# Three bias additions of GpSimd per graph, each in four pieces of 128x256 instead of one of 128x1024

## The chip, the cores and the metric

The kernel runs on one core of a Trainium2 chip, as one launch. The metric is the device time of the launch in microseconds (us). Three timed runs of the kernel before gave 2971.67, 2972.38 and 2974.36 us; the median is 2972.38 us. The profile that is read below is of one further execution.

## The reference

For each of 32 graphs there are node features `x` (512 nodes x 256, f32), an adjacency matrix `adj` (512x512, f32) and a node mask. Four graph layers follow each other, each with a residual and a layer norm:

```python
x = _layernorm(x + gin(x, adj))        # h = (1+eps)*x + adj@x; relu(h@W1 + b1)@W2 + b2
x = _layernorm(x + gat(x, adj))        # 4 heads, masked by adj > 0.5, softmax, ... + bias
x = _layernorm(x + attention(x, adj))  # 8 heads, scores + log(adj + 1e-6), softmax, (...)@Wo.T + bo
x = _layernorm(x + gnn3(x, mask, adj)) # (x@W)@x.T * adj, masked softmax, @x
```

The first three layers end in the addition of a row of 256 values: `b2`, `bias` and `bo`. These rows are the bias additions meant here. They are added to `x` itself, ahead of the layer's own result.

## The kernel before

**Tiling.** A graph's `x` is a tile of 128 partitions x 4 blocks x 256 columns, so node number c*128+p lies in block c of partition p. All of `x` is 128x1024 elements. The layers' matrices are held in transposed form where a matrix product needs them so. TensorE does all products and transposes, ScalarE (ACT in the profile) the exponentials and most copies out of PSUM, VectorE (DVE) the masking, statistics and residuals, GpSimd (POOL) the bias additions, the reciprocal square root of the norms, and the issue of accumulating DMAs between SBUF tiles. SyncE (SP) issues the loads and stores.

**Order.** Each graph is a list of named steps with an engine, an assumed duration, the steps that it comes after, and the buffers it takes. A planner (`Plan.order`) goes through the steps of all 32 graphs, up to six of them open at a time, and puts them into one order per engine by due times with hand-set shifts. The steps are then written out in that order, so every engine runs its own queue in order, and waits on semaphores of the others. Several graphs at different layers are in work at the same time: what stands next to each other on an engine is mostly of different graphs. The planner's assumed duration of a bias step is 2.5 us and is no part of the change.

**Names and lines used below.**
- L584, step `xb1`, `xb2`, `xb3` (one each per graph, `bias_steps(k, after)`): GpSimd adds row k-1 of `bias_bc` to all of `x`. `xb1` comes after the products that read `x` in layer 0 (L715, `hT_ps`), `xb2` after the transposes of `x` for layer 1 (L785, `xT_t`), `xb3` after those for layer 2 (L1057). The bias is added once nothing of the layer reads the plain `x` any more.
- L587 and L588: statistics of the norm, on VectorE. L604: `ve`, the variance plus epsilon, a 128x4 tensor-scalar operation on VectorE. L610: `rstd`, the power of -0.5 of it on GpSimd, 128x4. L618: `shift`, a 128x4 scalar-tensor-tensor operation on VectorE which needs `rstd`. L628: the normalization of `x` on ScalarE, which needs `shift`.
- L897: `edge`, the comparison of the transposed adjacency with 0.5, 128x512 f32 to uint8, on VectorE.
- L920: the combination of the layer-1 weights `z` with `T` and `edge`, 128x512, on VectorE. L943: the products that use `z` of layer 1 (`o_ps`).
- L1126: exponentials of layer 2 on ScalarE. L1135: their multiplication by the adjacency, 128x1024, on VectorE. L1171: the products that use them (`o_ps` of layer 2). L1113: the layer-2 scores.
- L971 and L1146: the accumulating DMAs that GpSimd issues.

Of the kernel before, what the change touches and what calls it, by code (L numbers as in the profile page):

```python
# [14 lines left out]
ALU = mybir.AluOpType  # L15
AX = mybir.AxisListType

P = 128
# [28 lines left out]
class Plan:  # L47
# [31 lines left out]
    def step(self, name, eng, us, after=(), take=(), free=(), mode=""):  # L79


        def add(emit):
            steps = self.steps[-1]
            known = {**steps, **{f"^{n}": s for n, s in self.steps[0].items()}}
            assert name not in steps and all(a in known for a in after), (name, after)
            takes = []
            for b in take:
                kind, _, key = b.partition("=")
                key, _, rest = key.partition("/")
                takes.append((kind, key or kind, int(rest or 0)))  # L90
            steps[name] = Step(eng, us, dict.fromkeys(after), takes, mode, emit)
            for b in free:
                self.free(b, (name,))
            return emit

        return add
# [131 lines left out]
def fast_path(  # L228
# [23 lines left out]
    nc = tc.nc  # L252
    B, N, D = x.shape
    NC = N // P
# [42 lines left out]
    bias_bc = const.tile([P, 3, D], F32, name="bias_bc")  # L297
# [259 lines left out]
    def graph(g):  # L557
# [3 lines left out]
        t = {"g": g}  # L561
# [16 lines left out]
        def bias_steps(k, after):  # L578


            @step(f"xb{k}", "pool", 2.5, after + ("^bias",))
            def _():
                b = bias_bc[:, k - 1, None, :].to_broadcast([P, NC, D])
                nc.gpsimd.tensor_tensor(t["x"], t["x"], b, ALU.add)  # L584

        def norm_stats(n, c):
            nc.vector.bn_stats(t[f"st{n}"][:, c, :], t["xo" if n == 4 else "x"][:, c, :])  # L587
# [1302 lines left out]
```

## Time and profile before

| what | value |
|---|---|
| median of the timed runs | 2972.38 us |
| the profiled execution, its own time | 2971.27 us |
| its span, first to last instruction | 2969.4 us |
| TensorE busy | 2943.3 us, 99% of the span |
| VectorE busy | 2150.4 us, 72% |
| ScalarE busy | 1927.3 us, 65% |
| GpSimd busy | 801.4 us, 27% |
| granted TensorE clock | 0.997 |
| bias additions | 96, shortest 2342 ns, median 2556 ns, longest 3246 ns |

The time of the execution is 1.9 us longer than its span. The span has a filling part at its start, when fewer graphs are open, a long middle part in which the same pattern of 91.3 us comes back for every graph, and a draining part. Profile lines have the start in us from the span's start, the duration in us, the engine, the line, the operation, the tiles (written <- read), their shapes, and, in brackets, the time that the engine sat idle before it and what ended the wait. A line with x2 or more merges instructions that follow each other.

### The profile page before, as it was taken

The numbers are of one execution on the slowest core, as the hardware profiler recorded it, in microseconds if no ns is written. First come the engines' busy times: TensorE is split into PE (matmuls) and PEld (weight loads), VectorE is DVE, ScalarE is ACT, GpSimd is POOL, SyncE is SP. The second block draws the span as 40 slices with busy tenths as digits, with TensorE's granted clock in tenths as the row PEclk, the third lists the DMA queues.
The fourth block names the chain that finished last, engine by engine and source line by source line (L and its number), as shares of the span: only waits on it lengthen the run. The fifth ranks groups of instructions, "written<-read, shape, count | busy, mean of one in ns | idle before, by whom it ended". The sixth has DMA issues, their size and how long they took to land.

```text
span 2969.4 us, 42791 instructions
## 1 busy us (share of the span) xinstructions
PE 2943.3 (99%) x15521; PEld 1668.0 (56%) x15521; DVE 2150.4 (72%) x4133; ACT 1927.3 (65%) x3818; POOL 801.4 (27%) x688
## 2 busy tenths in 40 slices
PE   8999999999999999999999999999999999999998
PEld 6545555555556555555555555555655555554545
DVE  3677777777777777677676777777777767767777
ACT  4666665667666676666676666766667666667664
POOL 1323222223232322222222222323232222223220
PEclk9999999999999999999999999999999999999999
DMA  4677766677766686666776666776668666677680
GB/s 146 137 156 174 165 153 140 145 158 169 166 146 140 140 183 162 154 134 143 176 165 155 137 148 156 170 166 146 139 140 185 159 156 133 142 176 157 138 178 16
DMA packets 153368, 448.93 MB, mean 151 GB/s; under 512 B 15232, under 2 KB 55360, under 8 KB 125248
## 3 DMA queue, kind: packets, MB, share of 16 engines
q0 software_dynamic: 63648, 295.73, 51.4%
q1 hardware_dynamic: 88112, 149.75, 15.4%
q8 instruction: 125, 2.05, 0.3%
q10 hardware_dynamic: 1392, 0.66, 0.1%
q14 instruction: 91, 0.75, 0.1%
HBM read 133.30 MB, written 17.07 MB: 51 GB/s over the span
## 4 chain that ended last, share of the span: by engine, by line
PE 85%; DVE 13%; DMA 1%; ACT 0%; issue 0%; POOL 0%; POOLq 0%; SPq 0%; ACTq 0%
PE h1T_ps L738 8%; PE s L1314 8%; PE hT_ps L715 8%; PE o_ps L1368 7%; PE y_ps L757 7%; PE o_ps L1171 6%; PE s L1113 6%; PE o_ps L943 5%; DVE z L1135 4%; PE v_ps L806 4%; PE v_ps L1094 4%; PE iT_ps L1300 4%; PE kT_ps L1076 4%; PE qT_ps L1076 4%; DVE st L587 2%; PE d_ps L1201 2%
## 5 line engine op out<-in xcount | busy, mean ns | idle before, releaser
L1126 ACT ACTIVATE z<-s 128x512 f32<-128x512 f32 x1024 | 551.3, 605 | 250.2 <-PE s L1113 250.0
L1135 DVE SCALAR_TENSOR_TENSOR z<-AT,z 128x1024 f32<-128x1024 f32 x512 | 625.6, 1241 | 95.7 <-ACT z L1126 93.0
L920 DVE SCALAR_TENSOR_TENSOR z<-z,T,edge 128x512 f32<-128x512 f32 x512 | 416.8, 857 | 38.2 <-ACT z L909 38.1
L1146 POOL DMA_DIRECT2D z<-z x186 | 164.1, 884 | 1005.5 <-DMA z<-z 358.7
L909 ACT ACTIVATE z<-R_bc,nT,S 128x512 f32<-128x512 f32 x512 | 376.6, 807 | 31.6 <-PE y_ps L757 22.4
L1220 DVE RECIPROCAL rdT<-rdT 128x256 f32<-128x256 f32 x128 | 215.9, 1725 | 188.3 <-ACT rdT L1213 188.3
L584 POOL TENSOR_TENSOR x<-x,bias_bc 128x1024 f32<-128x1024 f32 x96 | 245.2, 2555 | 395.0 <-PE xT_t L785 247.3
L971 POOL DMA_DIRECT2D z<-z x256 | 224.4, 970 | 457.0 <-DMA z<-z 168.4
L628 ACT ACTIVATE x<-x,shift,rstd 128x256 f32<-128x256 f32 x508 | 296.9, 600 | 52.1 <-DVE shift L618 51.5
L1171 PE MATMUL o_ps<-z,v 128*32 128x512 f32 x2048 | 295.3, 603 | 3.6 <-DVE z L1135 0.6
L1113 PE MATMUL s<-qT,kT 32*128 32x512 f32 x2048 | 288.1, 634 | 2.9 <-ACT qT L1082 2.9
L943 PE MATMUL o_ps<-z,v 128*64 128x512 f32 x1024 | 250.0, 609 | 2.7 <-DVE z L920 2.4
L738 PE MATMUL h1T_ps<-hT,w_sb 128*128 128x512 f32 x512 | 248.5, 610 | 0.0
L610 POOL TENSOR_TENSOR rstd<-ve,nhalf 128x4 f32<-128x4 f32 (+1 forms) x131 | 169.7, 1298 | 289.5 <-DVE ve L604 286.9
L1314 PE MATMUL s<-xT,iT 128*128 128x512 f32 x512 | 237.8, 599 | 0.0
L1368 PE MATMUL o_ps<-x,eT 128*128 128x256 f32 x1024 | 237.0, 379 | 0.1
L757 PE MATMUL y_ps<-w_sb,h1T 128*128 128x256 f32 x1024 | 230.8, 379 | 0.0
L757 PEld LDWEIGHTS y_ps<-w_sb,h1T 128*128 128x128 f32 x1024 | 194.2, 190 | 49.7 <-issue 25.8
L1368 PEld LDWEIGHTS o_ps<-x,eT 128*128 128x128 f32 x1024 | 193.8, 190 | 40.0 <-issue 13.6
L587 DVE BATCH_NORM_STATS2 st<-x 128x6 f32<-128x256 f32 x508 | 209.3, 412 | 4.7
L715 PE MATMUL hT_ps<-AT,x 128*128 128x384 f32 (+2 forms) x768 | 209.8, 382 | 0.0
L1113 PEld LDWEIGHTS s<-qT,kT 32*128 32x128 f32 x2048 | 87.2, 183 | 170.3 <-ACT z L1126 74.9
(152 smaller groups left out, 4236.8 us busy)
## 6 DMA issues: line engine op xcount, KB each, us to landing
z<-z POOLq DMA_DIRECT2D x186, 1024.0 KB, 8.7
A<-in_adj_dram SPq DMA_DIRECT2D x256, 256.0 KB
z<-z POOLq DMA_DIRECT2D x128, 512.0 KB, 5.5
R_bc<-R_dram SPq DMA_DIRECT2D x32, 1024.0 KB
z<-z POOLq DMA_DIRECT2D x128, 256.0 KB, 3.8
x<-in_x_dram SPq DMA_DIRECT2D x32, 512.0 KB
out_dram<-x SPq DMA_DIRECT2D x31, 512.0 KB
nm<-in_nodemask_dram SPq DMA_DIRECT2D x32, 256.0 KB
```

The costliest lines, as they stand in the source:

```text
L715: nc.tensor.matmul(ph[:, cols], t["x"][:, m, blk(d)], moving, start=(k == 0), stop=(k == len(parts) - 1),)
L738: nc.tensor.matmul(ph, w1_sb[:, d, blk(f)], t["hT"][:, d, :], start=(d == 0), stop=(d == DC - 1))
L757: nc.tensor.matmul(py[:, j, :], t["h1T"][:, f, blk(2 * c2 + j)], w2_sb[:, f, :], start=(f == 0), stop=(f == HC - 1),)
L909: nc.scalar.activation(t[f"e{h}"][:, c, :], t["Rbc"][:, h, :], AF.Relu, bias=t["nT"][:, h, c : c + 1], scale=t["S"][:, h, c : c + 1],)
L920: nc.vector.scalar_tensor_tensor(z, z, t["T"][:, h, c : c + 1], t["edge"][:, c, :], op0=ALU.add, op1=ALU.mult)
L943: nc.tensor.matmul(po[j * F1 : (j + 1) * F1, :], t["v"][:, c, h * F1 : (h + 1) * F1], t[f"e{h}"][:, c, :], start=(c == 0), stop=(c == NC - 1),
L1113: nc.tensor.matmul(pk, t["k"][hs, o, blk(c)], t["q"][hs, o, :], start=True, stop=True)
L1126: nc.scalar.activation(t[f"E{k}"][:, j, :], t[f"ps{k}{j}"], AF.Exp, scale=QSCALE)
L1135: nc.vector.scalar_tensor_tensor(z, t["AT"][:, c, None, :].to_broadcast([P, 2, N]), ADJ_EPS, z, op0=ALU.add, op1=ALU.mult,)
L1171: nc.tensor.matmul(t[f"n{o}"][32 * j : 32 * j + 32, :], t["v2"][:, c, o * P + F2 * j : o * P + F2 * (j + 1)], t[f"E{k}"][:, j, :], start=( ...
L1314: nc.tensor.matmul(pt, t["iT"][:, d, blk(c)], t["xT3"][:, d, :], start=(d == 0), stop=(d == DC - 1),)
L1368: nc.tensor.matmul(py, t[f"eT{c}"][:, blk(m)], t["x"][:, m, :], start=(m == 0), stop=(m == NC - 1),)
```

## The change

The one instruction of a bias step becomes a loop over the four blocks of `x`. Each piece reads and writes one block of 256 columns and reads the 256 values of the row directly, with no broadcast over blocks. The step keeps its name, its place, its predecessors and its assumed duration, so the planner gives the same order. Other lines move down by 3.

```diff
             @step(f"xb{k}", "pool", 2.5, after + ("^bias",))
             def _():
-                b = bias_bc[:, k - 1, None, :].to_broadcast([P, NC, D])
-                nc.gpsimd.tensor_tensor(t["x"], t["x"], b, ALU.add)
+
+                for c in range(NC):
+                    nc.gpsimd.tensor_tensor(
+                        t["x"][:, c, :], t["x"][:, c, :], bias_bc[:, k - 1, :], ALU.add
+                    )
```

In the built programs of this part GpSimd has 96 x 3 = 288 more additions. The four pieces stand where the one stood, and the order of all other instructions on all engines is the same. A piece waits for the last readers of its own block alone: for `xb2` and `xb3`, piece c waits for the transpose of block c, where the one addition waited for the transposes of all blocks. An instruction with several semaphores to wait for has a separate wait instruction ahead of it on its queue, and GpSimd has 235 more of those.

## Prediction

> **What bounds the kernel now.** I read the page first: busy times, the chain that ended last, and the row of the changed instruction.
>
> ```profile
> PE 2943.3 (99%) x15521; PEld 1668.0 (56%) x15521; DVE 2150.4 (72%) x4133; ACT 1927.3 (65%) x3818; POOL 801.4 (27%) x688
> ...
> PE 85%; DVE 13%; DMA 1%; ACT 0%; issue 0%; POOL 0%; POOLq 0%; SPq 0%; ACTq 0%
> ...
> L584 POOL TENSOR_TENSOR x<-x,bias_bc 128x1024 f32<-128x1024 f32 x96 | 245.2, 2555 | 395.0 <-PE xT_t L785 247.3
> ```
>
> TensorE is full, and GpSimd, which does the additions, is 27% busy and absent from the chain. That alone would say "no effect". But the chain runs through VectorE for 13% of the span, so I went through TensorE's timeline for places where a matmul starts later than the one before lets it. From 230 to 2700 us there is one such place, in every 91.3 us period. I read it in the graph around 1124 us, first GpSimd, then VectorE, then TensorE, each from its timeline.
>
> ```profile
> 1124.42 2.35 POOL L584 TENSOR_TENSOR x<-x,bias_bc 128x1024 f32<-128x1024 f32 x1 [8.50 <-PE xT_t L785]
> 1128.08 2.25 POOL L610 TENSOR_TENSOR rstd<-ve,nhalf 128x4 f32<-128x4 f32 x2 [1.31 <-DVE ve L604]
> ...
> 1124.77 2.02 DVE L604 TENSOR_SCALAR ve<-mv 128x4 f32<-128x4 f32 x1
> 1126.71 1.21 DVE L1135 SCALAR_TENSOR_TENSOR z<-AT,z 128x1024 f32<-128x1024 f32 x1
> 1127.85 0.16 DVE L604 TENSOR_SCALAR ve<-mv 128x4 f32<-128x4 f32 x1
> 1127.92 0.41 DVE L897 TENSOR_SCALAR edge<-AT 128x512 uint8<-128x512 f32 x1
> 1128.25 1.21 DVE L1135 SCALAR_TENSOR_TENSOR z<-AT,z 128x1024 f32<-128x1024 f32 x1
> 1129.39 0.41 DVE L897 TENSOR_SCALAR edge<-AT 128x512 uint8<-128x512 f32 x1
> 1129.72 0.15 DVE L618 SCALAR_TENSOR_TENSOR shift<-mv,rstd 128x4 f32<-128x4 f32 x1
> ...
> 1131.34 0.41 DVE L897 TENSOR_SCALAR edge<-AT 128x512 uint8<-128x512 f32 x1
> 1131.67 2.52 DVE L1135 SCALAR_TENSOR_TENSOR z<-AT,z 128x1024 f32<-128x1024 f32 x2
> ...
> 1131.80 0.60 PE L1171 MATMUL o_ps<-z,v 128*32 128x512 f32 x2
> ...
> 1132.94 1.05 PE L1171 MATMUL o_ps<-z,v 128*32 128x512 f32 x4
> ```
>
> The reader is to see two things. The first L604 works on 128x4 elements and takes 2.02 us, where the second takes 0.16: it stands still until the bias addition, which began 0.35 us earlier, ends at 1126.77. And from there to 1132.89 VectorE runs without a gap (each start lies some 0.08 us ahead of the end before), so the lost 1.9 us arrive whole at the first of the two L1135 at 1131.67. It ends at 1132.89, and the products that need it start 0.05 us later. The pair of matmuls before them started at 1132.23, and pairs of this line elsewhere follow each other by 0.42 us: TensorE loses 0.28 us. This repeats in 27 graphs, 27 x 0.28 = 7.6 us. Other steady waits of TensorE on VectorE have 0.4 us to spare or more. The stalls of the filling part, which add up to some 15 us, wait for layer chains where few graphs are open; I leave them as they are.
>
> **What the Trainium skill says.** "SBUF — State Buffer", section "Who interferes with whom": VectorE and GpSimd share a read and a write port, held for a whole instruction; an operation with two SBUF inputs, or a tensor-scalar operation in a two-port mode, blocks against a GpSimd operation that reads SBUF, and the one that started first holds. The trace agrees: L604 above, and L920 (0.74 us alone) takes 2.77 us in each `xb3`. Statistics (L587), with one input, lose nothing beside a bias addition. It also shows the other direction: at 252.72 us an addition waits for L920 and takes 2.94 us. "GPSIMD Engine Reference", section 3.1, gives 4497 ns for such an addition of 2048 columns. "Perfetto Trace Analysis", section "GPSIMD Engine Instruction", calls GpSimd spans unreliable and prefers start-to-start times; here the two bias additions that follow at 44.43 us take 4.67 us together, twice 2.36 less 0.05, so spans serve.
>
> **The change, part by part.**
>
> *Removed:* 96 additions of 2.35 us when undisturbed. *Added:* 384 pieces. The trace has no piece. With a fixed part f, a piece is f + (2352 - f)/4 = 588 + 0.75f ns. f is not below 0: 588 ns. An estimate for the upper end from the skill's 4497 ns and the 2352 here: slope (4497-2352)/1024 = 2.095 ns, f = 207, a piece 743 ns. The smallest GpSimd operations in the trace, fills of one column, take 97 to 102 ns; f = 100 gives 663. I take 700, so four take 4 x 0.70 - 3 x 0.05 = 2.65 us alone, 0.3 more than before. GpSimd, idle for 73% of the span, has room for it. The 235 added wait instructions are 17 ns each when fulfilled, and run ahead on the queue while the piece before works: nothing.
>
> *Moved:* the first piece may start three transposes earlier, 3 x 0.109 = 0.33 us before the addition did.
>
> *What matters is who gets the ports between pieces.* From the trace: a waiting addition gets them 0.14 us before the VectorE operation's end (252.72: 0.59 us of waiting, L920 ends at 0.72), ahead of VectorE's next, which already stood in line. VectorE gets them about 0.13 us before an addition's end. So they take turns. I write the place above out by hand, in us from 1124.42, with 0.57 us of ports per piece:
> - piece 1 from -0.33, piece 2 from 0.32; L604 waits until 0.89, the first L1135 follows at 0.97
> - piece 3 asks at 0.97 too. If VectorE is first: L1135 to 2.18, piece 3 from 2.10 to 2.80
> - L604 at 2.67, then at 2.75 L897 and piece 4 ask at the same moment. If VectorE is first: L897 to 3.16, piece 4 to 3.78, second L1135 from 3.65 to 4.86
> - GpSimd's L610 is queued behind piece 4. It begins at 3.73 and needs the ports, which the second L1135 holds to 4.72; then 1.03 us, so `rstd` is there at 5.8
> - L618 follows at 5.85. Before, it started at 5.30 (1129.72)
>
> Behind L618 everything stands in VectorE's queue: L897, L1135, L618, L897, and the L1135 for which TensorE waits. ScalarE also waits for it, at L628. From there nothing of the bias is left, and the rest follows as before, 0.55 us later. TensorE has no slack there, so it loses 0.55 us more per graph: 27 x 0.55 = 14.9 us. The profiled execution would become 2971.27 + 14.9 = 2986.2; the median lies 1.1 us above that execution, so 2987.
>
> The two bounds of a piece give, with the same turns, 0.1 us (588 ns) and 0.65 us (743 ns): 3 and 18 us. Turns are what decides. Both are near ties: an addition starts 0.05 us before the end of the one ahead (44.43 us), and VectorE's next operation starts 0.06 us before the end of an addition that blocked a short one (L1135 at 1126.71 against 1126.77). VectorE is ahead by 10 ns. In the trace a VectorE operation that starts 17 ns ahead wins (an L920 beside the addition at 252.72), one that starts 66 ns behind loses (L604 at 1763.93). Hence I let it win.
>
> *The other two places.* `xb1` runs mostly while VectorE idles; its first L1135 waits 0.2 to 0.6 us today, and the next is bound by ScalarE. `xb3` at 1183.47 blocks L920 for 2.03 us; with turns, three L920 and L1336 share the same sum of waits, the bias ends some 1.2 us later, and the DMA issues behind it start 1.5 us after its end today because they wait for L920. The products that use these results have 2 us to spare. I cost both at nothing; without that cover a wait of 0.3 us would be 8 us.
>
> **The rivals.**
> 1. *GpSimd wins one of the two ties.* Then piece 4 is done at 3.4 and L610 starts ahead of the second L1135, or just waits for L897; `rstd` is there at 4.7, VectorE reaches L618 at about 5.15 and TensorE's wait shrinks by 0.15 to 0.28 us, 4 to 7.6 us in all: about 2966. For it: the ties are within 10 ns, and a start in the record need not be the moment of the request. The gain can't be larger, since that wait is all there is.
> 2. *Nothing.* Total port time is about the same, pieces are near 588 ns and L618 moves by less than 0.1 us: 2972 to 2975. For it: GpSimd has 0% of the chain. Against: L610 has no more than 0.5 us to spare behind the bias.
> 3. *Pieces that wait longer.* If L1135 also comes between pieces 1 and 2 or wait instructions open gaps of 0.1 us, `rstd` comes a whole L1135 later, 1.1 us: 27 x 1.1 = 30 us, 3002.
>
> That the change doesn't do what it says is excluded by the built program: 288 more additions, the same order.
>
> **How the numbers follow.** Forecast (VectorE wins both ties) 0.58, rival 1 0.25, rival 2 0.13, rival 3 0.04. The likeliest gives 2987; its own range is 2979 to 2992. The range reaches to rival 1 at the lower end, 2965, and to 2994 above. A difference under 0.2%, 6 us, can't be told from none. Rival 1 gives 4 to 7.6 us: 0.14 of its 0.25 is counted as faster, 0.11 as the same. The same: 0.11 + 0.13. Slower: 0.58 + 0.04.
>
> **What would show it.** In the changed profile: pieces of 0.65 to 0.75 us with L1135 between the second and third and L897 before the fourth; L604 at 0.6 us or less; L618 of the middle graphs 5.8 us after the place of the old start; the wait of TensorE at the second L1171 pair grown from 0.28 to 0.8 us; a period of 91.85 us. L618 earlier than 5.3 us, or a fourth piece directly behind the third, makes the forecast wrong. So does a new wait of TensorE near `xb1` or `xb3`.

## The result and the profile after

The changed kernel takes 2989.28 us (median of 4 runs, 2988.76 to 2990.03); the kernel before took 2972.03 us beside it (4 runs, 2970.98 to 2974.36). The ratio is 1.0057, 95% interval 1.004 to 1.0075: slower by 0.57%. The profiled execution's span went from 2969.4 to 2988.2 us, by 18.8 us.

The page of the changed kernel: busy times, the chain, and two groups. A group's numbers are busy us, mean ns of one, and the idle us of the engine ahead of it, with what ended most of it.

```profile
PE 2949.8 (99%) x15521; PEld 1668.9 (56%) x15521; DVE 2152.0 (72%) x4133; ACT 1927.9 (65%) x3818; POOL 929.2 (31%) x976
...
PE 89%; POOL 4%; DVE 4%; issue 1%; DMA 1%; ACT 0%; POOLq 0%; SPq 0%; ACTq 0%
...
L585 POOL TENSOR_TENSOR x<-x,bias_bc 128x256 f32<-128x256 f32 x384 | 360.9, 1034 | 360.2 <-PE xT_t L788 241.9
...
L1174 PE MATMUL o_ps<-z,v 128*32 128x512 f32 x2048 | 303.6, 603 | 13.9 <-DVE z L1138 13.9
```

GpSimd, with 0% of the chain before, now has 4%. Its busy time grew by 128 us, but that is no measure of the damage: the records include waits for the ports, and GpSimd still idles for 69% of the span. The products L1174 (L1171 before) idled 3.6 us in the old profile, 0.6 us of it for `z`, and now 13.9 us, all for `z`.

Both programs have the same 15521 matmuls in the same order. So I compared, one by one, the time from each matmul to the next, and summed the differences by their place in the period of 91.3 us, for the steady 27 graphs. Only two places lose: the products behind `xb2`, 10.7 us, and the products behind `xb1`, 8.4 us. The filling and the draining part gain 0.2 and 0.5 us.

**Behind `xb2`.** The timeline of the changed kernel in one graph, GpSimd, VectorE and TensorE together; L607 is L604 of before, L613 is L610, L621 is L618, L1138 is L1135, L900 is L897.

```profile
1222.15 4.09 POOL L585 TENSOR_TENSOR x<-x,bias_bc 128x256 f32<-128x256 f32 x4 [8.92 <-PE xT_t L788]
...
1222.93 0.67 DVE L607 TENSOR_SCALAR ve<-mv 128x4 f32<-128x4 f32 x1
...
1223.51 1.21 DVE L1138 SCALAR_TENSOR_TENSOR z<-AT,z 128x1024 f32<-128x1024 f32 x1
...
1224.65 0.69 DVE L607 TENSOR_SCALAR ve<-mv 128x4 f32<-128x4 f32 x1
...
1225.24 0.41 DVE L900 TENSOR_SCALAR edge<-AT 128x512 uint8<-128x512 f32 x1
...
1225.58 1.74 DVE L1138 SCALAR_TENSOR_TENSOR z<-AT,z 128x1024 f32<-128x1024 f32 x1
...
1226.20 3.00 POOL L613 TENSOR_TENSOR rstd<-ve,nhalf 128x4 f32<-128x4 f32 x2
...
1228.25 0.16 DVE L621 SCALAR_TENSOR_TENSOR shift<-mv,rstd 128x4 f32<-128x4 f32 x1 [0.59 <-POOL rstd L613]
...
1230.23 2.51 DVE L1138 SCALAR_TENSOR_TENSOR z<-AT,z 128x1024 f32<-128x1024 f32 x2
...
1231.49 1.05 PE L1174 MATMUL o_ps<-z,v 128*32 128x512 f32 x4 [0.50 <-DVE z L1138]
```

The reader is to see the turns. The four pieces start at 1222.15, 1222.85, 1223.53 and 1225.27; the third waits while L1138 has the ports, and the fourth while L900 has them. The first L613 starts only behind the fourth, meets the second L1138, and takes 2.01 us instead of 1.03. VectorE now has a gap of 0.59 us ahead of L621, where before it had none. What follows is as before, later, and the last products wait.

**Behind `xb1`.** The timeline of before, then of the changed kernel, for the same graph.

```profile
1239.47 0.86 POOL L1146 DMA_DIRECT2D z<-z  x1 [10.84 <-issue]
...
1240.03 2.68 POOL L584 TENSOR_TENSOR x<-x,bias_bc 128x1024 f32<-128x1024 f32 x1
...
1242.07 5.14 DVE L1135 SCALAR_TENSOR_TENSOR z<-AT,z 128x1024 f32<-128x1024 f32 x4 [1.89 <-ACT z L1126]
...
1246.64 1.92 PE L1171 MATMUL o_ps<-z,v 128*32 128x512 f32 x16
```

```profile
1246.95 0.86 POOL L1149 DMA_DIRECT2D z<-z  x1 [11.09 <-issue]
...
1247.51 3.09 POOL L585 TENSOR_TENSOR x<-x,bias_bc 128x256 f32<-128x256 f32 x4
...
1249.31 5.79 DVE L1138 SCALAR_TENSOR_TENSOR z<-AT,z 128x1024 f32<-128x1024 f32 x4 [1.89 <-ACT z L1129]
...
1253.89 2.32 PE L1174 MATMUL o_ps<-z,v 128*32 128x512 f32 x16
```

Here the bias addition starts 0.30 us before the DMA issue ahead of it ends. There are no turns at all: the four pieces are through in 3.09 us, at 1250.60, and the first L1138, which asked at 1249.31, takes 2.38 us and ends 1.09 us after them. The sixteen products stretch from 1.92 to 2.32 us.

### The profile page after: what moved, and what is told of

Same layout as the page of the kernel before. It is cut to its first block, busy times and chain, and to the rows that moved or that the text cites. A ratio compares the mean times of both kernels' runs of the same rounds, so it can differ in the third digit from the quotient of the medians.

```text
span 2988.2 us, 43288 instructions
## 1 busy us (share of the span) xinstructions
PE 2949.8 (99%) x15521; PEld 1668.9 (56%) x15521; DVE 2152.0 (72%) x4133; ACT 1927.9 (65%) x3818; POOL 929.2 (31%) x976
## 4 chain that ended last, share of the span: by engine, by line
PE 89%; POOL 4%; DVE 4%; issue 1%; DMA 1%; ACT 0%; POOLq 0%; SPq 0%; ACTq 0%
PE h1T_ps L741 8%; PE s L1317 8%; PE o_ps L1174 8%; PE hT_ps L718 8%; PE o_ps L1371 7%; PE y_ps L760 7%; PE s L1116 7%; PE o_ps L946 4%; PE v_ps L809 4%; PE v_ps L1097 4%; PE iT_ps L1303 4%; PE o2p_ps L1259 4%; PE kT_ps L1079 4%; PE qT_ps L1079 4%; DVE z L1138 2%; POOL x L585 2%
## 5 line engine op out<-in xcount | busy, mean ns | idle before, releaser
L1138 DVE SCALAR_TENSOR_TENSOR z<-AT,z 128x1024 f32<-128x1024 f32 x512 | 653.8, 1297 | 92.8 <-ACT z L1129 89.5
L585 POOL TENSOR_TENSOR x<-x,bias_bc 128x256 f32<-128x256 f32 x384 | 360.9, 1034 | 360.2 <-PE xT_t L788 241.9
L1149 POOL DMA_DIRECT2D z<-z x186 | 163.7, 882 | 972.3 <-DMA z<-z 363.7
L923 DVE SCALAR_TENSOR_TENSOR z<-z,T,edge 128x512 f32<-128x512 f32 x512 | 387.5, 800 | 35.8 <-ACT z L912 35.7
L1174 PE MATMUL o_ps<-z,v 128*32 128x512 f32 x2048 | 303.6, 603 | 13.9 <-DVE z L1138 13.9
L613 POOL TENSOR_TENSOR rstd<-ve,nhalf 128x4 f32<-128x4 f32 (+1 forms) x131 | 188.2, 1440 | 270.1 <-DVE ve L607 255.3
L1371 PEld LDWEIGHTS o_ps<-x,eT 128*128 128x128 f32 x1024 | 193.8, 190 | 39.7 <-issue 13.9
```

The lines of the kernel that those rows point to most:

```text
L585: nc.gpsimd.tensor_tensor(t["x"][:, c, :], t["x"][:, c, :], bias_bc[:, k - 1, :], ALU.add)
L923: nc.vector.scalar_tensor_tensor(z, z, t["T"][:, h, c : c + 1], t["edge"][:, c, :], op0=ALU.add, op1=ALU.mult)
L1138: nc.vector.scalar_tensor_tensor(z, t["AT"][:, c, None, :].to_broadcast([P, 2, N]), ADJ_EPS, z, op0=ALU.add, op1=ALU.mult,)
L1174: nc.tensor.matmul(t[f"n{o}"][32 * j : 32 * j + 32, :], t["v2"][:, c, o * P + F2 * j : o * P + F2 * (j + 1)], t[f"E{k}"][:, j, :], start=( ...
L1371: nc.tensor.matmul(py, t[f"eT{c}"][:, blk(m)], t["x"][:, m, :], start=(m == 0), stop=(m == NC - 1),)
```

## The experiments

All are made from the kernel before; "before" beside them had 2972.3 to 2972.6 us. In their profiles the lines are shifted; names in the text are those of before.

| kernel | us, median | ratio to before, 95% interval | TensorE behind `xb2` | behind `xb1` |
|---|---|---|---|---|
| changed kernel | 2989.28 | 1.0057 (1.0040 to 1.0075) | +10.7 us | +8.4 us |
| `xb2` alone in four pieces | 2983.59 | 1.0039 (1.0026 to 1.0053) | +10.8 | +2.1 |
| `xb1` alone in four pieces | 2975.68 | 1.0011 (1.0005 to 1.0018) | -0.3 | +3.6 |
| `xb3` alone in four pieces | 2971.71 | 0.9998 (0.9990 to 1.0006) | -0.3 | 0.0 |
| all three in halves | 2965.89 | 0.9980 (0.9972 to 0.9988) | -6.0 | +0.7 |
| `xb2` as 256 + 768 | 2963.59 | 0.9970 (0.9958 to 0.9982) | -7.5 | +0.3 |
| `xb2` in pieces behind `rstd` | 3003.02 | 1.0104 (1.0089 to 1.0120) | -20.2 | +43.3 |
| `xb2` in one piece, later | 2952.42 | 0.9933 (0.9920 to 0.9947) | -31.4 | +1.4 |
| `xb2` in four pieces, later | 2961.72 | 0.9960 (0.9947 to 0.9974) | -31.4 | -0.1 |
| `xb1` in pieces, its DMA issue behind it | 2970.72 | 0.9994 (0.9985 to 1.0002) | -0.2 | -0.1 |
| `xb1` in pieces, small addition ahead | 2975.82 | 1.0010 (1.0003 to 1.0016) | -0.3 | +6.6 |

The two right columns are the sums of TensorE's differences against the profile of before, made as above. They leave out the filling part, which varies by up to 2.4 us and is 4.1 to 5.9 us longer in the three kernels that move `xb2`, and the products L715, which lose 6.9 and 17.7 us in the two kernels with `xb2` later and nothing in the others.

**One place at a time.** Three kernels, each with this edit for one k (here `xb2`):

```diff
             def _():
+                if k == 2:
+                    for c in range(0, NC, 1):
+                        b = bias_bc[:, k - 1, None, :].to_broadcast([P, 1, D])
+                        part = t["x"][:, c : c + 1, :]
+                        nc.gpsimd.tensor_tensor(part, part, b, ALU.add)
+                    return
                 b = bias_bc[:, k - 1, None, :].to_broadcast([P, NC, D])
```

> Only the second bias addition of a graph (xb2) in four pieces. Theory (the rstd waits behind piece 4, and the second L1135 keeps the ports from it): the stall of TensorE behind z at the second L1171 goes from 0.28 to 0.67 us in each graph, as in the changed kernel, so about +10 us, 2982 to 2983. Rival (every piece costs GpSimd a fixed time, and each of the three additions bears a third of the loss): +5.8 us, 2978.

> Only the first bias addition (xb1) in four pieces. Theory (its pieces follow a DMA issue so closely that they overlap and don't give the ports back, and L1135 is kept out until all four have ended, 0.6 us later than before, with about 0.3 us to spare): +8 us, 2980, with new waits of 0.3 us behind z at L1171 in some 20 of 27 graphs, and the stall after xb2 still 0.28 us. My forecast's reckoning (2 us to spare): 0, 2972. Rival (a third each): +5.8 us.

> Only the third bias addition (xb3) in four pieces. Theory: its place has neither a product nor a rstd that is late, so 0 within 1.5 us. Rival (a third each): +5.8 us, 2978.

`xb2` alone costs 11.3 us and `xb3` nothing, as expected; the rival of a price per piece falls, since the same 96 added pieces cost 11.3 us, 3.4 us and nothing. `xb1` alone costs 3.4 us and not 8, with 14 losing graphs of the 21 compared below, not 20 of 27: the three sum up to 14.1 us, against 17 for the whole change. 2.7 us of the missing 3.2 are at the products behind `xb1`, where the two changes make each other's harm worse (8.4 us together, 2.1 and 3.6 alone). I took the 21 steady graphs in which `xb1` of before starts within the DMA issue ahead of it or right at its end (in the other six it starts 0.19 to 0.56 us later), and counted its start and end from one fixed matmul, 30 ahead of `xb1` in TensorE's order:

| kernel | start of `xb1`, median | duration | end | graphs in which TensorE loses over 0.05 us | sum of 21 |
|---|---|---|---|---|---|
| before | 4.92 us | 2.68 us | 7.60 us | - | - |
| `xb2` in pieces | 5.15 | 2.68 | 7.83 | 8 | 2.1 us |
| `xb1` in pieces | 4.94 | 3.08 | 8.02 | 14 | 3.6 us |
| changed kernel | 5.15 | 3.08 | 8.24 | 19 | 8.4 us |

Two shifts, 0.23 us (`xb1` starts later when `xb2` is in pieces; the DMA issue behind `xb2` and `rstd`, 0.24 us after the first L1171 products before, comes 0.98 us after them in the changed kernel) and 0.40 us (four pieces are longer than one). TensorE's loss is a plain difference: in 18 of the 19 losing graphs of the changed kernel it is the end of `xb1` less 7.85 us to within 0.04 us (in 17, to 0.005), for example 8.042: 0.191, 8.238: 0.392, 8.639: 0.794. Before, the median end was 7.60. So the products there had 0.25 us to spare; either shift alone stays mostly inside it, and both together do not.

**Halves.** The same edit for all k, in steps of two blocks:

```diff
+                if True:
+                    for c in range(0, NC, 2):
+                        b = bias_bc[:, k - 1, None, :].to_broadcast([P, 2, D])
+                        part = t["x"][:, c : c + 2, :]
+                        nc.gpsimd.tensor_tensor(part, part, b, ALU.add)
+                    return
```

> All three additions in two pieces of 128x512. Theory: a half takes about 1.27 us (estimated between 0.72 for 256 and 2.35 for 1024 columns), L1135 gets the ports after the first half, and the rstd behind the second half comes before the second L1135 has asked, so L618 starts no later than 5.3 us and the stall of 0.28 us shrinks or goes; after xb1 the wait of L1135 is at most one half. So 0 to -7 us, 2965 to 2972. Rival (loss grows with the number of pieces, +17 for nine added): three added, +6 us, 2978.

It came as expected, 6.4 us faster than before; the rival falls. A half took 1.27 us at the start of `xb2`. The timeline of this kernel at that place (L610 is L604 of before, L616 is L610, L624 is L618, L1141 is L1135):

```profile
1212.54 3.55 POOL L587 TENSOR_TENSOR x<-x,bias_bc 128x512 f32<-128x512 f32 x2 [9.12 <-PE xT_t L791]
...
1213.14 0.70 DVE L610 TENSOR_SCALAR ve<-mv 128x4 f32<-128x4 f32 x1
...
1213.75 1.21 DVE L1141 SCALAR_TENSOR_TENSOR z<-AT,z 128x1024 f32<-128x1024 f32 x1
...
1216.27 2.19 POOL L616 TENSOR_TENSOR rstd<-ve,nhalf 128x4 f32<-128x4 f32 x2 [0.17 <-DVE ve L610]
...
1216.37 1.21 DVE L1141 SCALAR_TENSOR_TENSOR z<-AT,z 128x1024 f32<-128x1024 f32 x1
...
1217.85 0.15 DVE L624 SCALAR_TENSOR_TENSOR shift<-mv,rstd 128x4 f32<-128x4 f32 x1
```

`rstd` starts at 1216.27, 0.10 us ahead of the second L1141, and takes its 1.08 us undisturbed. With four pieces it starts 0.62 us behind that instruction, and has to wait for it. L624 starts 5.30 us after the bias addition, as before (1129.72 less 1124.42); but the addition started 0.25 us sooner (0.60 us ahead of the first L610, where the old one was 0.35 ahead of L604), and TensorE gains 0.24 to 0.26 us in 24 of the 27 graphs.

**An early first piece, without a pause in the middle.**

```diff
+                if k == 2:
+                    for c, n in ((0, 1), (1, 3)):
+                        b = bias_bc[:, k - 1, None, :].to_broadcast([P, n, D])
+                        part = t["x"][:, c : c + n, :]
+                        nc.gpsimd.tensor_tensor(part, part, b, ALU.add)
+                    return
```

> xb2 in two pieces, of 256 and of 768 columns; xb1 and xb3 in one piece. Theory (a first piece waits for the transposes of its own rows alone, so the work starts 0.3 to 0.4 us earlier; the rest follows before VectorE has asked for the ports): the rstd and L618 come 0.2 to 0.4 us earlier, the stall of 0.28 us goes, -5 to -7 us, 2965 to 2967. Rival (it is the pause in the middle, where L1135 takes the ports, that helped the halves): no pause here, so 2972 or above.

9.0 us faster than before, 0.27 us per graph behind `xb2`: slightly more than expected, and without the rival's pause, as the second piece follows 0.69 us after the first. The first piece starts 0.77 us ahead of the first L604 (0.35 before), and the addition ends 1.73 us after L604's start, where it was 2.00: the 0.27 us.

**The same pieces behind `rstd`.** The edit of `xb2` in four pieces, and in the finished order of each graph but the first `xb2` moves behind the next two GpSimd steps:

```diff
+        out = self.order(*best[1])[1]
+        for g in range(1, len(self.steps)):
+            at = next(i for i, s in enumerate(out) if s[:2] == (g, "xb2"))
+            moved, left = out.pop(at), 2
+            while left and not (out[at][0] == g and "xb2" in self.steps[g][out[at][1]].after):
+                left -= self.steps[out[at][0]][out[at][1]].eng == "pool"
+                at += 1
+            out.insert(at, moved)
```

> xb2 in four pieces as in the run of xb2 alone, but moved behind the two rstd (L610) on GpSimd; xb1 and xb3 in one piece. Theory (the loss at that place is the rstd's wait behind the pieces, not the pieces): L604 and the rstd come about 2 us earlier, the stall of 0.28 us at the second L1171 goes, -6 us there; the L1146 behind the pieces comes some 2.8 us later, and so may xb1, which costs up to 0.4 us in each of 27 graphs where it happens. Between 2964 and 2974, against 2983.6 for the same pieces ahead of the rstd. Rival (the pieces themselves cost, by their ports or their number): no better than 2980.

A miss in the time: 3003.0 us. At the place itself the theory held: 20.2 us won, against 10.8 lost with the pieces ahead of `rstd`. But the products behind `xb1` lose 43.3 us. The timeline of this kernel (L1149 is L1135, L1160 is L1146; L624 is the `rstd`):

```profile
1140.15 2.24 POOL L624 TENSOR_TENSOR rstd<-ve,nhalf 128x4 f32<-128x4 f32 x2 [10.20 <-PE o_ps L957]
...
1142.37 5.99 POOL L595 TENSOR_TENSOR x<-x,bias_bc 128x256 f32<-128x256 f32 x4
...
1144.34 5.09 DVE L1149 SCALAR_TENSOR_TENSOR z<-AT,z 128x1024 f32<-128x1024 f32 x3
...
1148.30 0.91 POOL L1160 DMA_DIRECT2D z<-z  x1
...
1163.78 0.86 POOL L1160 DMA_DIRECT2D z<-z  x1 [12.93 <-issue]
...
1163.97 4.14 DVE L1149 SCALAR_TENSOR_TENSOR z<-AT,z 128x1024 f32<-128x1024 f32 x1 [1.89 <-ACT z L1140]
...
1164.34 2.68 POOL L598 TENSOR_TENSOR x<-x,bias_bc 128x1024 f32<-128x1024 f32 x1
```

The pieces take turns with three L1149 and need 5.99 us instead of the 2.8 us that I reckoned with. The DMA issue behind them comes 4.31 us after the first L1171 products, where it came 0.24 us after them before. The third L1160 of the graph adds up what the two ahead of it bring. Those two now stand 1.7 us apart and not 6, and the second lands 13.3 us after its issue, at 1163.26, where it took 11.2 us at this place before. The third is issued 0.52 us after that landing, as before, and `xb1`, right behind it, starts about 2.5 us later than before and keeps an L1149 out for 2.9 us. What is queued behind the moved instruction weighed more than what it made room for.

**`xb2` in one piece, later.** Nothing is split; the same move, past four GpSimd steps instead of two (`left` = 4), behind both `rstd` and two DMA issues.

> xb2 in one piece, moved behind both rstd and the two L1146 issues after them, where GpSimd idles for 10 us; nothing is split. Theory: the stall of 0.28 us goes (-6 to -7 us), and the third L1146 and xb1 stay where they are: 2965 to 2967. Rival (the stall of 0.28 us is not the bias addition's): 2972.

2952.4 us, 20 us faster than before and 13 more than expected. The timeline of this kernel (L618 is the `rstd`, L626 L618, L1179 L1171, L1154 L1146, L828 an addition of two SBUF tiles in layer 1, L696 and L700 the addition and the copy that take the transposed adjacency out of PSUM in layer 0, L723 the products L715, which wait for L700):

```profile
1122.60 2.24 POOL L618 TENSOR_TENSOR rstd<-ve,nhalf 128x4 f32<-128x4 f32 x2 [10.20 <-DVE ve L612]
...
1126.44 1.06 PE L1179 MATMUL o_ps<-z,v 128*32 128x512 f32 x8
...
1128.19 1.04 PE L1179 MATMUL o_ps<-z,v 128*32 128x512 f32 x8
...
1131.62 0.86 POOL L1154 DMA_DIRECT2D z<-z  x1 [5.91 <-DVE rd L1021]
...
1132.18 2.68 POOL L592 TENSOR_TENSOR x<-x,bias_bc 128x1024 f32<-128x1024 f32 x1
...
1133.79 1.16 DVE L828 TENSOR_TENSOR ab<-v,ab_off 128x32 f32<-128x32 f32 x1
...
1135.15 1.56 ACT L700 COPY AT<-AT_t 128x512 f32<-128x512 f32 x3 [0.66 <-DVE ATd L696]
```

The second eight products are the point. In the profile of before they are these two lines of the timeline, the first eight products of the place and the second:

```profile
1130.05 1.07 PE L1171 MATMUL o_ps<-z,v 128*32 128x512 f32 x8
...
1131.80 2.19 PE L1171 MATMUL o_ps<-z,v 128*32 128x512 f32 x8
```

The same eight records (two for each of four heads) took 2.19 us before and 1.04 us here. Their starts show why: before, they start in twos (at 1131.80, 1132.23, 1132.94 and 1133.39), because `z` of the first two heads was there and that of the others came only at 1132.89; here `z` of all four was there from 1127.48 on, and they start in fours, at 1128.20 and 1128.62. TensorE's busy time falls from 2943.3 to 2920.3 us with no matmul less. So 1.15 us per graph were to be had, of which only 0.28 showed as a stall. A part goes back at L715: 0.12 to 0.14 us in 25 of the 27 graphs and 3.8 us in one, 6.9 us in all. The moved addition keeps L828 out, which takes 1.16 us instead of 0.21, and the L696 and L700 behind it are late. (The wait of 0.34 us that the next expectation names overstates this.)

**`xb2` later, in four pieces.** The move of the last kernel with the edit of the first.

> xb2 behind both rstd and two L1146 issues, as in the run where it was moved in one piece (2952.4), but now in four pieces; it stands directly behind a DMA issue there. Theory (pieces behind a DMA issue overlap and hold the ports to the last): the whole takes 3.1 instead of 2.68 us, VectorE's two-input operations stay out until its end, L696 and with it the products at L723 come 0.4 us later in each graph: about +11 us, 2963. Rival (pieces give the ports back between them wherever VectorE waits): L696 gets in after a piece, the wait of 0.34 us there shrinks, 2943 to 2952.

9.3 us slower than the same move in one piece, near the expected 11. The timeline of this kernel (L834 is L828 of the last):

```profile
1134.83 0.86 POOL L1160 DMA_DIRECT2D z<-z  x1 [5.92 <-DVE rd L1027]
...
1135.39 3.09 POOL L595 TENSOR_TENSOR x<-x,bias_bc 128x256 f32<-128x256 f32 x4
...
1136.79 0.30 DVE L702 TENSOR_TENSOR ATd<-AT_t,selfw 128x128 f32<-128x128 f32 x1 [2.34 <-PE AT_t L696]
...
1136.99 1.57 DVE L834 TENSOR_TENSOR ab<-v,ab_off 128x32 f32<-128x32 f32 x1
```

Again a DMA issue directly ahead, 3.09 us for the four, and an operation of VectorE that is kept out to their end at 1138.48: 1.57 us, where it took 1.16 behind one addition. L702 (L696), with one input in PSUM, runs undisturbed in between. TensorE loses 0.40 us more per graph at L715.

**Is it the DMA issue ahead?** `xb1` in pieces, with the DMA issue moved behind it:

```diff
+            at = next(i for i, s in enumerate(out) if s[:2] == (g, "xb1"))
+            dma = next((i for i in range(at - 1, -1, -1) if self.steps[out[i][0]][out[i][1]].eng == "pool"), None)
+            if dma is not None and out[dma][1][:2] == "cd":
+                out.insert(at, out.pop(dma))
```

> xb1 in four pieces, with the L1146 issue that stood directly ahead of it moved behind it; xb2 and xb3 in one piece. Theory (pieces that start during a DMA issue overlap and hold the ports without a break): now each piece takes 0.72 us and L1135 gets the ports after the piece that runs when it asks, so that it waits 0.7 us at most instead of to the end of the last piece. Rival (the pieces overlap whatever is ahead): L1135 still ends 1.09 us after the last piece. The time itself can go either way, since that L1146 is issued up to 3 us later: 2966 to 2985.

And `xb1` in pieces with a small addition between the DMA issue and the first:

```diff
+                    pad = little([P, NC], "pad")
+                    nc.gpsimd.tensor_tensor(pad, nhalf, nhalf, ALU.add)
```

> xb1 in four pieces with one more small GpSimd addition (128x4, its result is not used) between the L1146 issue and the first piece. Theory (what makes the pieces overlap is that the first starts before the DMA issue has ended): if the small addition takes up that overlap, the pieces behind it are 0.72 us each and L1135 gets the ports between two of them, before the last has ended. Rival (the overlap is passed on from instruction to instruction, or has nothing to do with the DMA): the pieces' records stay at 1.04 us and L1135 ends 1.09 us after the last. The time: 0.1 to 0.8 us later in each graph than without the small addition where L1135 stays out, 2978 to 2995.

In the first, 2970.7 us, each piece takes 0.72 us, but they are over before L1135 asks (they end 5.4 us after the fixed matmul, it asks at 6.95), so the question of the turns was not put; the place costs nothing. In the second the rival's forecast of the records came true: the small addition itself starts 0.30 us before the DMA issue ends, the pieces' records stay at 1.02 to 1.06 us, 0.68 us apart, and the L1135 of the graph at 1242 us ends 1.09 us after the last. Being separated from the DMA issue by an instruction does not end the overlap. The forecast of the time was missed: 2975.8 us is below 2978 to 2995, and level with the 2975.7 us without the small addition.

The changed kernel's own filling part has the comparison that these two runs did not make, an `xb2` directly behind an issue L1149 and not into it:

```profile
144.14 0.86 POOL L1149 DMA_DIRECT2D z<-z  x1 [5.75 <-PE s L1116]
145.04 4.14 POOL L585 TENSOR_TENSOR x<-x,bias_bc 128x256 f32<-128x256 f32 x4
...
145.24 1.61 DVE L1138 SCALAR_TENSOR_TENSOR z<-AT,z 128x1024 f32<-128x1024 f32 x1 [1.64 <-ACT z L1129]
```

The first piece starts 0.04 us after the issue has ended. L1138 asks 0.20 us later and is through at 146.85, between the first piece and the second. Over all traces with four pieces, take the bias steps in which VectorE asks before the last piece starts and is held up by more than 0.2 us. Where the first instruction of the step starts 0.29 us or more before the end of a DMA issue, VectorE gets in only behind the last piece, in 74 of 75 steps; in all 160 others, which start at most 0.06 us before such an end, it gets in between two pieces.

## Why the prediction came out as it did

The time was forecast at 2987 us and came at 2989.3. The two numbers are closer than the reasoning deserves, and part of that is luck: the term behind `xb2` was 4.2 us too large (14.9 against 10.7), and one of 8.4 us behind `xb1` was missing. The forecast had named "a new wait of TensorE near `xb1` or `xb3`" as a sign of being wrong, and there is one near `xb1`.

*Right: the mechanism behind `xb2`, step by step.* A piece was put at 0.70 us and is 0.72; four alone at 2.65 us and 2.78, with starts 0.69 us apart. The first piece starts 0.42 us sooner against L604, where 0.33 was reckoned. L1135 comes between pieces two and three and L897 before piece four: the two near ties went to VectorE, each by a start 23 ns ahead. The first L604 takes 0.67 us (0.6 or less was forecast), and TensorE's wait grows from 0.28 to 0.67 us (to 0.8 was forecast). `rstd` is held up by the second L1135, as the hand-written list had it. Where the pieces stand, and not that they are pieces, decides: behind `rstd` the same pieces win 20.2 us at that place.

*Mis-sized: "27 x 0.55 = 14.9 us".* It measured 0.39 to 0.42 us per graph in 26 of 27, 10.7 us. On the list's scale L618 starts at 5.69 (the median) instead of 5.85: the first piece is 0.1 us earlier, and the second L1135 ends at 4.76 and not 4.86.

*Wrong: "The products that use these results have 2 us to spare. I cost both at nothing".* For `xb3` nothing was right. For `xb1` it was 8.4 us. The spare time was 0.25 us, so the "0.4 us to spare or more" that the prediction gives TensorE's other waits fails here too, and two things that I had not carried through ate it: the first L1135 is kept out until the last piece ends, 0.40 us later, and `xb1` itself starts 0.23 us later, since the DMA issues behind `xb2`'s late `rstd` are late. The setting could be read before: the old timeline shows `xb1` starting 0.56 us into a DMA issue, and the blocked L1135 ending 1.09 us after it. That pieces would take no turns there could not be read from it, since it has no pieces. The warning that I wrote beside it, "without that cover a wait of 0.3 us would be 8 us", is what happened.

*Wrong: "The gain can't be larger, since that wait is all there is"*, said of the rival in which GpSimd wins a tie. The 7.6 us of stalls are not all there is. The eight products in twos hold 1.15 us per graph, about 31 us, and the kernel with `xb2` later gets them. Halves do come out at the rival's time, 2965.9 against 2966, with `rstd` ahead of the second L1135 as the rival has it; but no tie decides there, so the same number is a coincidence.

The rival "nothing", with its argument that GpSimd has 0% of the chain, is refuted by `xb2` alone in pieces.

## What to carry to other kernels

Splitting an instruction that holds a shared resource helps or hurts by what stands next in both queues, so write out the turns for each place where it occurs, and follow the instructions queued behind the pieces, DMA issues included, to their next consumer. A cover is a number to be measured (here 0.25 us where 2 us were assumed), and two shifts that each fit into it may not fit together. A TensorE that is 99% busy may still have time to give: look for products that could run side by side and start in twos.

## What the runs showed of the hardware

- The Trainium skill, "SBUF — State Buffer", section "Who interferes with whom", has the shared ports held for a whole instruction, and the other engine blocked until then. The runs agree where the first piece does not start into a DMA issue, whether GpSimd had waited before it or came straight from `rstd`: turns after each piece or two. Where the first piece starts in the last 0.30 us of a DMA issue, they go further: the pieces' records last 1.02 to 1.06 us with starts 0.69 us apart, and a waiting VectorE operation gets in only behind the last, in the changed kernel, in `xb1` alone, at `xb2` moved behind such an issue, and with a small addition between. (Halves have the longer records there too, 1.58 to 1.60 us, but VectorE asks there only during the second.) The start into the issue goes with the missing turns in 74 steps of 75, and without it there were turns in 160 of 160, one of them directly behind such an issue. No run shows what happens inside GpSimd, so that part stays open, as does the one exception, where the first piece starts 0.64 us before the issue ends.
- One addition of 128x1024 takes 2.35 us alone and 2.68 us when it starts into such an issue; 128x512 took 1.27 us, 128x256 0.72 us.
